# Pinning VectorE operations, five buffers for q, and other queues for some transfers in a four-layer convolution network

## The chip, the cores and the metric

The program runs on one core of one Trainium2 chip. The metric is device time in microseconds from start to end of the program, the median over several executions. Lower is better. All data are float32 except where a table says bf16.

## The reference

Input x is (4, 256, 64, 64). Four layers follow each other, each of the form x + layer(groupnorm(x)); only the first and the preparation of weights for the others concern the change.

```python
# layer 0: axial attention over rows, N = B*H rows, 16 groups, 16 channels each
qkv = einsum('nci,oc->noi', xp, w_qkv)
qkv = bn(qkv)                       # statistics over all rows and positions
qe  = einsum('ngci,cij->ngij', q, q_emb)
ke  = einsum('ngci,cij->ngij', k, k_emb)
qk  = einsum('ngki,ngkj->ngij', qe, ke)
sim = bn(concat([qk, qe, ke]))      # again statistics over everything
sim = softmax(sim summed over its three parts)
attn   = einsum('ngij,ngcj->ngci', sim, v)
attn_e = einsum('ngij,cij->ngci', sim, v_emb)
out = bn(concat([attn, attn_e])) summed in pairs
# layer 1: 3x3 convolution, weights made ternary with a threshold
delta = 0.7 * mean(abs(w));  w_t = where(w > delta, 1, where(w < -delta, -1, 0)) * alpha
# layer 2: two grouped 3x3 convolutions of sign(x), batch norms, residuals
# layer 3: 3x3 convolution whose weights are w * a / (1 + exp(w * b)) for 16 pairs (a, b)
```

## The kernel before

The kernel is written in a tile language. The author writes operations for an engine (VectorE, ScalarE, TensorE, GpSimd, and the queues that issue transfers: SyncE, ScalarE, GpSimd). A scheduler then decides the order of each engine's instructions from estimated durations, mostly the earliest written among those that it holds to be ready, and adds the waits on semaphores. On the chip every engine runs its list in order. A pool hands out tiles; tiles of one tag share so many buffers, and a new tile waits until the last reader of its buffer is done.

The span has three stages ahead of the convolutions.

**Stage A** (the first `with` block, lines 160 to 340) goes over four images b and eight chunks k of 512 positions. `normalised(b)` loads an image in four pieces (SyncE), takes its statistics (L192, VectorE) and yields mean and scale; it is written at chunk 4 of the image before. For each chunk VectorE writes the normalised columns `xg` (L259), TensorE makes q and k rows (`po`, L267) and v columns (`pv`, L282), ScalarE copies them out, VectorE takes statistics of `po` (L274). q and k go to DRAM as `q_d` (L308, SyncE, 16 stores after each image), v as `vt_d` (ScalarE). Beside this the weights of layer 1 are made: `threshold` sums the absolute weights over six pieces (L229), written for b = 0, k = 6; `ternary(i)` (L240 to L250) loads a piece again, compares it (L245, L246), and `kernel_rows` makes six combinations that are stored as `u1_d`, two pieces for each of the images 1 to 3. Both loads and the store are issued by GpSimd, from one buffer.

**Stage B** (lines 365 to 629) goes over 16 tiles j of q and k (4 images, 4 sets of groups). `projections(j)` loads a tile `qb` of 1 MB from `q_d` in two transfers on SyncE (L405) and scales it with four VectorE instructions (L411). There are three buffers; the tile for j + 2 is asked for when tile j begins. A tile takes two group pairs gp, each with four steps: 64 small matmuls `pd` (L446), two VectorE transposes of them into `t` (L453), and, for the step before, 64 small matmuls `pq` (L465) in `product`, copied and squared by ScalarE (L469, L474). After each gp, `term_sums` reduces the tile (L421 to L423), makes a matrix product `ptq` (L426) and multiplies it with the tile (L431), all for batch-norm sums. Between the tiles ten jobs make the weights of layers 3 and 2: `weights_3` (six: exponentials on ScalarE, L488 to L490 and `kernel_rows` on VectorE, a store L496) and `weights_2` (four: loads L502 or L506, sums and splitting into bf16 parts L513 to L522, a store L523). They are written one after each tile from tile 0 on; their transfers are SyncE's.

**Stage C** (lines 633 to 905) goes over eight units. `scores` loads `qc` (L693) and `si` (L711) on SyncE, ScalarE scales qc (L699), TensorE makes `e` (L723), VectorE adds `si` (L735), ScalarE takes exponentials (L765), TensorE sums them (L776) and then makes the values `pa` (L808) and `pe` (L832). `load_values` (L679) fetches the v tiles `vb`, 16 transfers a unit in four parts, each written after the two value products that read the old content; ScalarE issues them.

Of the kernel before, what the change touches and what calls it, by code (L numbers as in the profile page):

```python
# [17 lines left out]
P = 128  # L18
B = 4
# [19 lines left out]
def network(ctx: ExitStack, tc, x, wqkv, relm, relt, relw, relv, counts, masks, vecs, rowv, ab, w1, l2w1, l2w2, l3w, mats, out):  # L39
# [116 lines left out]


    bqh = ctx.enter_context(ExitStack())
    bqp = pool(bqh, "b_q", 3, side="right")
    with ExitStack() as ph:  # L160
        wp = pool(ph, "a_w")
        xp_ = pool(ph, "a_x", 6)
# [57 lines left out]
        delta = sp.tile([P, 2], F32, name="delta")  # L220

        def weights_1(i, name):
            w = kp.tile([P, 3, C], F32, name=f"{name}_{i}", tag="w")
            nc.gpsimd.dma_start(out=w, in_=w1[i])
            return w

        def threshold():
            for i in range(len(pieces)):
                nc.vector.tensor_reduce(  # L229
                    sizes[:, i : i + 1], weights_1(i, "wa").rearrange("p a o -> p (a o)"), AX.X, ALU.add,  # L230
                    apply_absolute_value=True,
                )
            s = small(sp, [P, 1])
            nc.vector.tensor_reduce(s, sizes, AX.X, ALU.add)
            ps = pst.tile([P, 1], F32, name="pdelta", tag="pst")
            nc.tensor.matmul(ps, lhsT=mt[:, M_ALL, :], rhs=s, start=True, stop=True)
            nc.vector.tensor_scalar(delta[:, 0:1], ps, 1.0 / (2 * 9 * C), 0.7, ALU.mult, ALU.mult)
            nc.vector.tensor_scalar(delta[:, 1:2], delta[:, 0:1], -1.0, None, ALU.mult)

        def ternary(i):  # L240
            t, dx = pieces[i]
            w = weights_1(i, "wb")
            alpha = row[:, 96:97]
            up = kp.tile([P, 3, C], F32, name=f"up_{i}", tag="up")
            nc.vector.tensor_scalar(up, w, delta[:, 0:1], alpha, ALU.is_gt, ALU.mult)  # L245
            nc.vector.tensor_scalar(w, w, delta[:, 1:2], alpha, ALU.is_lt, ALU.mult)  # L246
            nc.vector.tensor_tensor(w, up, w, ALU.subtract)
            u = kp.tile([P, 6, C], F32, name=f"u1_{i}", tag="u")
            kernel_rows(u, w, up[:, 0], up[:, 1])
            nc.gpsimd.dma_start(out=u1_d[:, t, dx], in_=u)  # L250

        ready = normalised(0)
        for b in range(B):
            xs, gm, rs = ready
            qs = [qp.tile([P, 8, 8, 64], F32, name=f"qs{t}_{b}", tag="qs") for t in range(2)]
            for k in range(NB):
                xg = gp_.tile([P, 2, 512], F32, name=f"xg_{b}_{k}", tag="xg")
                for t in range(2):
                    nc.vector.tensor_scalar(  # L259
                        xg[:, t, :], xs[t][k // 4][:, bass.ts(k % 4, 512)], gm[:, t : t + 1], rs[:, t : t + 1],  # L260
                        ALU.subtract, ALU.mult,
                    )
                for o in range(2):
                    ps = psp.tile([P, 8, 64], F32, name=f"po_{b}_{k}_{o}", tag="po", bufs=3)
                    psf = ps.rearrange("p h w -> p (h w)")
                    for t in range(2):
                        nc.tensor.matmul(  # L267
                            psf, lhsT=wt[:, t, bass.ts(o, P)], rhs=xg[:, t, :], start=(t == 0), stop=(t == 1)
                        )
                    nc.scalar.copy(  # L270
                        qs[o][:, :, :, bass.ts(k, 8)].rearrange("p l a h -> p h a l"),
                        ps.rearrange("p h (a l) -> p h a l", l=8),
                    )
                    nc.vector.bn_stats(st1[:, o, b * NB + k, :], psf)  # L274
                if k % 2 == 0:
                    vs = vp.tile([P, C, 8], F32, name=f"vs_{b}_{k}", tag="vs")
                for half in range(2):
                    pv = psp.tile([P, 2, C], F32, name=f"pv_{b}_{k}_{half}", tag="pv")
                    for j in range(2):
                        pix = bass.ts(2 * half + j, P)  # L280
                        for t in range(2):
                            nc.tensor.matmul(  # L282
                                pv[:, j, :], lhsT=xg[:, t, pix], rhs=wt[:, t, C : 2 * C],
                                start=(t == 0), stop=(t == 1),
                            )
                    c = 4 * (k % 2) + 2 * half
                    nc.scalar.copy(vs[:, :, c : c + 2], pv.rearrange("p j c -> p c j"))
                    sq = jp.tile([P, 2, C], F32, name=f"vq_{b}_{k}_{half}", tag="vq")
                    nc.scalar.activation(sq, pv, AF.Square)
                    squares.append((b, 2 * k + half, sq))  # L290
                    if len(squares) > 4:
                        for _ in range(4):
                            add_squares()
                if k % 2 == 1:
                    for r in range(2):
                        nc.scalar.dma_start(
                            out=vt_d[b][k // 2, r].rearrange("p a c m -> p a (c m)"),
                            in_=vs.rearrange("p (a r c) m -> p r a (c m)", r=2, c=16)[:, r],
                        )
                if k == 4 and b + 1 < B:  # L300
                    ready = normalised(b + 1)
                if b == 0 and k == 6:
                    threshold()
                if b > 0 and k in (1, 5):
                    ternary(2 * (b - 1) + k // 4)
            for t in range(2):
                for l in range(8):
                    nc.sync.dma_start(  # L308
                        out=q_d[b][l, t].rearrange("c g f -> g c f"), in_=qs[t][:, l].rearrange("p a h -> p (a h)")
                    )  # L310
# [53 lines left out]
    cqp = pool(cih, "c_q", 3)  # L364
    with ExitStack() as ph:
        rp = pool(ph, "b_r")
        tp_ = pool(ph, "b_t", 2)
        op = pool(ph, "b_o", 2)
        jp = pool(ph, "b_j", 2)
# [30 lines left out]
        def projections(j):  # L400

            b, s = divmod(j, 4)
            q = bqp.tile([P, 4, 8, 64], F32, name=f"qb_{j}", tag="qb")
            for t in range(2):
                nc.sync.dma_start(  # L405
                    out=q[64 * t : 64 * t + 64].rearrange("p g a n -> p (g a n)"),
                    in_=q_d[b][:, t, :, 4 * s : 4 * s + 4].rearrange("l c g f -> l c (g f)"),
                )
            for g in range(4):
                c = 4 * s + g  # L410
                nc.vector.tensor_scalar(  # L411
                    q[:, g], q[:, g], sq[:, 0, c : c + 1], sq[:, 1, c : c + 1], ALU.mult, ALU.add
                )
            return q

        def term_sums(j, q, half):

# [63 lines left out]
        def weights_3(t, dx):  # L481
# [11 lines left out]
            u = kp.tile([P, 6, C], F32, name=f"u3_{t}_{dx}", tag="u3")  # L493
            ef = e.rearrange("p r a o -> p (r a o)")
            kernel_rows(u, w, ef[:, 0:C], ef[:, C : 2 * C])
            nc.sync.dma_start(out=u3_d[:, t, dx], in_=u)  # L496

        def weights_2(i, g):

            w = kp.tile([P, 9, 64], F32, name=f"w2_{i}_{g}", tag="w2")  # L500
            if i == 0:
                nc.sync.dma_start(out=w, in_=l2w1[:, g])  # L502
            else:

                for two in range(2):
                    nc.sync.dma_start(out=w[64 * two : 64 * two + 64], in_=l2w2[g][:, two])  # L506
            w3 = w.rearrange("p k o -> p (k o)").rearrange("p (a n) -> p a n", a=3)
            u = kp.tile([P, 4, 3 * 64], F32, name=f"u2_{i}_{g}", tag="u2")
            t = kp.tile([P, 3 * 64], F32, name=f"t2_{i}_{g}", tag="t2")
# [9 lines left out]
            for j in range(3):  # L519
                v.tensor_copy(parts[:, j], uf)  # L520
                if j < 2:
                    v.tensor_tensor(uf, uf, parts[:, j], ALU.subtract)  # L522
            nc.sync.dma_start(out=bk_d[i][:, g], in_=parts)  # L523

        jobs = [(weights_3, (t, dx)) for t in range(2) for dx in range(3)]
        jobs += [(weights_2, (i, g)) for i in range(2) for g in range(2)]
# [17 lines left out]
                whole.append((b, gp, o, 0))  # L544

        last = None
        qs = [projections(0), projections(1)]
        for b in range(B):
            for gp in range(GP):
                j = 4 * b + gp // 2  # L550
                if gp % 2 == 0 and j + 2 < 4 * B:
                    qs.append(projections(j + 2))
                q = qs[0]
                o = op.tile([P, 32, 64, 2], F32, name=f"o_{b}_{gp}", tag="o")
                for nb in range(2):
                    ts = [tp_.tile([P, 16, 64, 2], F32, name=f"t{t}_{b}_{gp}_{nb}", tag=f"t{t}") for t in range(2)]
# [4 lines left out]
                            finish(last, 2 * jh + 1)  # L561
                    last = (ts, o, b, gp, nb)
                term_sums(j, q, gp % 2)
                if gp % 2 == 1:
                    qs.pop(0)
                    if jobs:
                        job, args = jobs.pop(0)
                        job(*args)
        for k in range(4):
# [99 lines left out]
    def attention(general, good):  # L669
# [5 lines left out]
        def load_values(u, m):  # L675
            b, th = units[u]
            for r in range(2):
                for h in range(2):
                    nc.scalar.dma_start(  # L679
                        out=vb[m][64 * r : 64 * r + 64, h, :, 16 * r : 16 * r + 16, :]  # L680
                        .rearrange("p a c m -> p a (c m)"),
                        in_=vt_d[b][m, r, 64 * h : 64 * h + 64, 4 * th : 4 * th + 4]
                        .rearrange("p a c m -> p a (c m)"),
                    )
# [895 lines left out]
```

## Time and profile before

| | |
|---|---|
| time, median of 3 runs | 3115.93 us (3112.61 to 3126.57) |
| span of the profiled execution | 3128.6 us |
| TensorE matmul busy | 2623.8 us (84%) |
| VectorE busy | 2063.7 us (66%) |
| ScalarE busy | 1120.8 us (36%) |
| GpSimd busy | 55.4 us (2%) |
| moved by DMA | 484.05 MB, mean 155 GB/s |

In the profile PE is TensorE's matmul, PEld its weight load, DVE VectorE, ACT ScalarE, POOL GpSimd, SP SyncE; a q behind a name (SPq, ACTq) is the engine's queue of instructions that issue transfers. L411 is line 411 of the kernel. A row of a timeline gives the start and the duration in us, engine, line, operation, output <- input, the number of merged instructions, and in brackets the idle time of the engine before it with what ended it. A row of waits names the waiting engine and line, who released it, the total in us, how often, and the longest.

### The profile page before, as it was taken

Reading aid. Unit: us, or ns where it says so; the run is one execution under the profiler, and the core shown is the slowest. Engines: PE = TensorE matmul, PEld = TensorE weight load, DVE = VectorE, ACT = ScalarE, POOL = GpSimd, SP = SyncE. Lnnn points to the kernel's source line nnn. Section 1 sums busy time; section 2 is a strip of 40 time slices with the busy share of each in tenths; the row PEclk is TensorE's granted clock in tenths of the full one; section 3 lists DMA queues with packets and bytes.
Section 4 is the critical chain, followed back from the end, with each engine's and each line's share of the span. In section 5 each row is a group of like instructions: output and inputs, shape, how many; then the busy total and the mean of one; then the engine's idle time right before and its main releaser. Section 6 shows DMA issues by size and latency. Waiting matters only on the chain. (4 is left out here: it accounts for less than half of the span.)

```text
span 3128.6 us, 82568 instructions
## 1 busy us (share of the span) xinstructions
PE 2623.8 (84%) x36800; PEld 1593.2 (51%) x36800; DVE 2063.7 (66%) x3554; ACT 1120.8 (36%) x2201; POOL 55.4 (2%) x119
## 2 busy tenths in 40 slices
PE   5789778878888777777773699999996885999998
PEld 3456556656666656655663344444453452444443
DVE  5653897655655545555566888877597768778653
ACT  2445344444445465555541010101267931101010
POOL 0000000000000000000000000000000000000000
PEclk9989889889889988999997899999998997999999
DMA  5765354333233567776766444340434644443200
GB/s 187 246 202 158 120 193 154 116 110 128 107 110 124 145 198 236 249 246 227 243 206 225 127 155 151 102 151 28 158 121 166 233 165 151 134 133 116 88 40 41
DMA packets 246522, 484.05 MB, mean 155 GB/s; under 512 B 27344, under 2 KB 127056, under 8 KB 226320
## 3 DMA queue, kind: packets, MB, share of 16 engines
q1 hardware_dynamic: 147872, 335.02, 32.5%
q10 hardware_dynamic: 96464, 134.24, 12.3%
q0 software_dynamic: 1824, 9.44, 0.9%
q8 instruction: 291, 4.77, 0.6%
q14 instruction: 71, 0.58, 0.1%
HBM read 282.28 MB, written 196.35 MB: 153 GB/s over the span
## 5 line engine op out<-in xcount | busy, mean ns | idle before, releaser
L971 PE MATMUL gc<-gtr,g_u 128*128 128x512 f32 x1152 | 500.2, 596 | 21.2 <-issue 13.0
L971 PE MATMUL dc<-dtr,d_u 128*128 128x512 f32 x1152 | 502.7, 597 | 17.6 <-DVE dtr L957 12.0
L446 PE MATMUL pd<-rm,qb 64*32 64x256 f32 x8192 | 296.8, 408 | 92.5 <-DVE t L453 87.7
L453 DVE STREAM_TRANSPOSE t<-pd 128x1024 f32<-128x1024 f32 x256 | 304.4, 1226 | 102.0 <-PE pd L446 101.1
L971 PEld LDWEIGHTS gc<-gtr,g_u 128*128 128x128 f32 x1152 | 218.1, 190 | 295.4 <-issue 281.7
L971 PEld LDWEIGHTS dc<-dtr,d_u 128*128 128x128 f32 x1152 | 217.4, 190 | 288.8 <-issue 264.5
L465 PEld LDWEIGHTS pq<-t,t 64*64 64x64 f32 x8192 | 266.0, 139 | 81.9 <-issue 52.4
L465 PE MATMUL pq<-t,t 64*64 64x64 f32 x8192 | 285.3, 223 | 24.5 <-issue 17.3
L1203 PE MATMUL pc<-e_tr,e_k 128*64 128x512 bf16 x2304 | 266.0, 392 | 38.6 <-ACT pc_o L1211 19.9
L469 ACT ACTIVATE o<-pq 128x512 f32<-128x512 f32 x256 | 152.2, 595 | 390.2 <-PE pq L465 389.9
L446 PEld LDWEIGHTS pd<-rm,qb 64*32 64x32 f32 x8192 | 161.9, 113 | 180.5 <-DVE t L453 102.5
L765 ACT ACTIVATE pt<-pt,sm 128x512 f32<-128x512 f32 x256 | 162.5, 708 | 188.8 <-DVE pt L735 111.4
L1203 PEld LDWEIGHTS <-e_k 128*64 128x64 bf16 x2304 | 152.2, 112 | 151.2 <-issue 49.6
L735 DVE TENSOR_TENSOR pt<-e_False,si_False 128x1024 f32<-128x1024 f32 x128 | 150.5, 1217 | 60.7 <-PE e_False L723 60.6
L776 PE MATMUL den_False<-pt,cnt 128*32 128x128 f32 x2048 | 118.3, 302 | 55.9 <-ACT pt L765 32.4
L474 ACT ACTIVATE pq<-pq 128x512 f32<-128x512 f32 x256 | 149.5, 584 | 5.9
L267 PE MATMUL po<-xg,wt 128*128 128x512 f32 x256 | 126.3, 633 | 23.4 <-DVE st L274 20.3
L989 ACT COPY gc_c<-gc 128x512 f32<-128x512 f32 x32 | 18.6, 581 | 343.8 <-PE gc L971 343.8
L989 ACT COPY dc_c<-dc 128x512 f32<-128x512 f32 x32 | 18.7, 584 | 329.2 <-PE dc L971 329.2
L723 PE MATMUL e_False<-qc_False,rw 32*64 32x256 f32 x2048 | 111.5, 422 | 21.9 <-ACT qc_False L699 11.9
L808 PE MATMUL pa_False<-pt,vb 128*32 128x64 f32 x4096 | 103.0, 240 | 27.5 <-issue 23.0
L832 PE MATMUL pe_False<-pt,ve 128*32 128x64 f32 x4096 | 91.3, 233 | 39.6 <-issue 33.0
(379 smaller groups left out, 3437.5 us busy)
## 6 DMA issues: line engine op xcount, KB each, us to landing
si_False<-qk_d SPq DMA_DIRECT2D x64, 1024.0 KB
qk_d<-o ACTq DMA_DIRECT2D x124, 512.0 KB
x<-x_d SPq DMA_DIRECT2D x32, 1056.0 KB
a<-at_d SPq DMA_DIRECT2D x256, 128.0 KB
xa<-in_x SPq DMA_DIRECT2D x16, 1024.0 KB
vt_d<-vs ACTq DMA_DIRECT2D x32, 512.0 KB
q_d<-qs SPq DMA_DIRECT2D x64, 256.0 KB
qb<-q_d SPq DMA_DIRECT2D x32, 512.0 KB
```

The costliest lines, as they stand in the source:

```text
L267: nc.tensor.matmul(psf, lhsT=wt[:, t, bass.ts(o, P)], rhs=xg[:, t, :], start=(t == 0), stop=(t == 1))
L446: nc.tensor.matmul(pds[t][32 * c : 32 * c + 32, m].rearrange("p j k -> p (j k)"), lhsT=q[rows, 2 * (gp % 2) + g, a, 32 * nb : 32 * nb + 32 ...
L453: nc.vector.transpose(ts[t][:, :, 32 * jh : 32 * jh + 32].rearrange("p a j b -> p j a b"), pds[t].rearrange("p m j k -> p j m k"),)
L465: nc.tensor.matmul(ps[rows, m, :], lhsT=ts[1][rows, n // 2, :, n % 2], rhs=ts[0][rows, n // 2, :, n % 2], start=True, stop=True, tile_posi ...
L469: nc.scalar.activation(o[:, :, 8 * k : 8 * k + 8, :], ps.rearrange("p n (a b) -> p a n b", b=2), AF.Copy, accum_out=acc[:, 0, gp, col : co ...
L474: nc.scalar.activation(psf, psf, AF.Square, accum_out=acc[:, 1, gp, col : col + 1])
L723: nc.tensor.matmul(es[x_ // 2][64 * r : 64 * r + 64, x_ % 2, :, :, par], lhsT=rw[rows, par, 63 - i : 127 - i], rhs=q[rows, :, k % 2, :].re ...
L735: nc.vector.tensor_tensor(dst, e, src, ALU.add)
L765: nc.scalar.activation(s, s, AF.Exp, scale=s2q[:, gp : gp + 1])
L776: nc.tensor.matmul(dens[u, h][32 * a : 32 * a + 32], lhsT=ones[:, i, :], rhs=pt[:, 16 * h + i, a].rearrange("p n b -> p (n b)"), start=(i ...
L971: nc.tensor.matmul(ms[k], lhsT=u[:, t, dx, k, bass.ts(co, P)], rhs=vs[t][:, k, :, dx : dx + 64], start=(first and dx == 0), stop=(last and ...
L1203: nc.tensor.matmul(m[64 * g : 64 * g + 64], lhsT=parts[:, g, i, k, dx, :], rhs=vs[g][:, k, 8 * (q % 2) : 8 * (q % 2) + 8, dx : dx + 64], s ...
```

## The change

The change touches stages A, B and C; what is computed stays.

- **Pins.** `tc.keep_in_program_order` holds a VectorE instruction at its written place in the engine's order. It is put around the four scalings of a q tile, the six reductions for the threshold, and the first comparison of each ternary piece.
- **q tiles.** Five pools of one buffer each, used by turns, in place of one pool of three; two of the five lie in stage B's own memory. Loads are asked for three tiles ahead, and the scaling of tile j + 1 is written in the middle of tile j, after `term_sums` of its first half.
- **Layer 1's weights.** Each reduction is written for its own chunk (k = 2 to 7 of image 0), the pieces have two buffers and are loaded by SyncE; those for `ternary` are loaded two chunks ahead of their use.
- **Weights of layers 2 and 3.** Their jobs begin after tile 3 rather than tile 0, and their loads and stores in the loop are issued by GpSimd.
- **Value loads** of stage C are issued by SyncE.

It is meant to keep VectorE from standing in front of a load, and the queues of SyncE and ScalarE from standing in front of transfers that wait.

```diff
-    bqp = pool(bqh, "b_q", 3, side="right")
+    bqps = [pool(bqh, f"b_q{i}", side="right") for i in range(3)]
...
         def weights_1(i, name):
-            w = kp.tile([P, 3, C], F32, name=f"{name}_{i}", tag="w")
-            nc.gpsimd.dma_start(out=w, in_=w1[i])
+            w = kp.tile([P, 3, C], F32, name=f"{name}_{i}", tag="w", bufs=2)
+            nc.sync.dma_start(out=w, in_=w1[i])
             return w
-        def threshold():
-            for i in range(len(pieces)):
+        def threshold(i):
+            w = weights_1(i, "wa")
+            tc.keep_in_program_order(
                 nc.vector.tensor_reduce(
-                    sizes[:, i : i + 1], weights_1(i, "wa").rearrange("p a o -> p (a o)"), AX.X, ALU.add,
+                    sizes[:, i : i + 1], w.rearrange("p a o -> p (a o)"), AX.X, ALU.add,
                     apply_absolute_value=True,
                 )
+            )
+            if i + 1 < len(pieces):
+                return
...
+        pieces_1 = {}
         def ternary(i):
-            w = weights_1(i, "wb")
+            w = pieces_1[i]
...
-            nc.vector.tensor_scalar(up, w, delta[:, 0:1], alpha, ALU.is_gt, ALU.mult)
+            tc.keep_in_program_order(
+                nc.vector.tensor_scalar(up, w, delta[:, 0:1], alpha, ALU.is_gt, ALU.mult)
+            )
...
-                if b == 0 and k == 6:
-                    threshold()
+                if b == 0 and 1 < k:
+                    threshold(k - 2)
                 if b > 0 and k in (1, 5):
                     ternary(2 * (b - 1) + k // 4)
+                if k in (3, 7) and 2 * b + k // 4 - 1 in range(len(pieces)):
+                    i = 2 * b + k // 4 - 1
+                    pieces_1[i] = weights_1(i, "wb")
...
+        bqps += [pool(ph, f"b_q{i}") for i in range(3, 5)]
...
-            q = bqp.tile([P, 4, 8, 64], F32, name=f"qb_{j}", tag="qb")
+            q = bqps[j % 5].tile([P, 4, 8, 64], F32, name=f"qb_{j}", tag="qb")
...
+            return q
+        def scaled(j, q):
             for g in range(4):
-                c = 4 * s + g
-                nc.vector.tensor_scalar(
-                    q[:, g], q[:, g], sq[:, 0, c : c + 1], sq[:, 1, c : c + 1], ALU.mult, ALU.add
+                c = 4 * (j % 4) + g
+                tc.keep_in_program_order(
+                    nc.vector.tensor_scalar(
+                        q[:, g], q[:, g], sq[:, 0, c : c + 1], sq[:, 1, c : c + 1], ALU.mult, ALU.add
+                    )
                 )
-            return q
...
-            nc.sync.dma_start(out=u3_d[:, t, dx], in_=u)
+            nc.gpsimd.dma_start(out=u3_d[:, t, dx], in_=u)
...
-                nc.sync.dma_start(out=w, in_=l2w1[:, g])
+                nc.gpsimd.dma_start(out=w, in_=l2w1[:, g])
...
-                    nc.sync.dma_start(out=w[64 * two : 64 * two + 64], in_=l2w2[g][:, two])
+                    nc.gpsimd.dma_start(out=w[64 * two : 64 * two + 64], in_=l2w2[g][:, two])
...
-            nc.sync.dma_start(out=bk_d[i][:, g], in_=parts)
+            nc.gpsimd.dma_start(out=bk_d[i][:, g], in_=parts)
...
-        qs = [projections(0), projections(1)]
+        qs = [projections(j) for j in range(3)]
+        scaled(0, qs[0])
         for b in range(B):
             for gp in range(GP):
                 j = 4 * b + gp // 2
-                if gp % 2 == 0 and j + 2 < 4 * B:
-                    qs.append(projections(j + 2))
-                q = qs[0]
+                if gp % 2 == 0 and j + 3 < 4 * B:
+                    qs.append(projections(j + 3))
+                q = qs[j]
...
                 term_sums(j, q, gp % 2)
+                if gp % 2 == 0 and j + 1 < 4 * B:
+                    scaled(j + 1, qs[j + 1])
                 if gp % 2 == 1:
-                    qs.pop(0)
-                    if jobs:
+                    if j > 2 and jobs:
                         job, args = jobs.pop(0)
                         job(*args)
...
-                    nc.scalar.dma_start(
+                    nc.sync.dma_start(
                         out=vb[m][64 * r : 64 * r + 64, h, :, 16 * r : 16 * r + 16, :]
```

## The prediction

> **What bounds the kernel now.** I read the page first (PE 84% busy, DVE 66%: neither is full), then cut the span by the first and last start of each line's instructions: stage A (projections of x) 0 to 333.6 us, stage B (position terms, products) 333.6 to 1076.9, stage C (attention) to 1690, then the convolutions, which the change leaves alone. All is decided in A to C, so I asked for the waits and stretches there. First the waits of stage B (waiting engine and line, releaser: us in total, times, longest), then those of SyncE's queue:
>
> ```profile
> PEld pd L446 <- DVE t L453: 102.5, 29, 9.0
> DVE t L453 <- PE pd L446: 101.1, 81, 2.5
> DVE qb L411 <- DMA qb<-q_d: 100.3, 13, 9.6
> PE pd L446 <- DVE t L453: 87.7, 25, 8.5
> ...
> SPq L405 <- DVE pr L431: 352.6, 13, 45.4
> SPq L496 <- DVE u L153: 66.1, 4, 24.7
> ```
>
> TensorE waits for transposes (L453), VectorE for the load of q (L411), and the load for a free buffer, which the last `pr` of tile j-1 gives back. VectorE is in order, so transposes queue behind the waiting scaling. The timeline shows one such round:
>
> ```profile
> 629.74 2.38 DVE L453 STREAM_TRANSPOSE t<-pd 128x1024 f32<-128x1024 f32 x2 [0.48 <-PE pd L446]
> 641.72 1.91 DVE L411 TENSOR_SCALAR qb<-qb,sm 128x512 f32<-128x512 f32 x4 [9.60 <-DMA qb<-q_d]
> ...
> 638.50 1.17 PE L465 MATMUL pq<-t,t 64*64 64x64 f32 x31 [3.74 <-issue]
> 644.85 3.65 PE L446 MATMUL pd<-rm,qb 64*32 64x256 f32 x60 [4.37 <-DVE t L453]
> ```
>
> The load is issued at 629.34 and lands 12 us later; after the gap 60 matmuls take 3.65 us, elsewhere 64 take 1.96. What a round costs is seen in the stretches: a tile with a load, and one of the last three, whose scaling is done:
>
> ```profile
> 688.60:735.20 46.60, 37.46 (x1040) 28.78 (x1040) 26.28 (x42) 20.91 (x64) 0.00 (x0) 0.90 0.33 115
> 1001.60:1037.00 35.40, 35.40 (x1044) 27.96 (x1041) 21.91 (x33) 20.91 (x64) 0.00 (x0) 1.00 0.32 122
> ```
>
> (us, then busy PE, PEld, DVE, ACT, POOL, granted clock.) Without the wait PE is full. In stage A, VectorE waits for weight pieces, and at 209 for x, and PE with it:
>
> ```profile
> 30.18 0.95 DVE L229 TENSOR_REDUCE sizes<-wa 128x1 f32<-128x768 f32 x1 [4.00 <-DMA wa<-in_w]
> ...
> 126.05 0.68 DVE L245 TENSOR_SCALAR up<-wb,delta,row 128x768 f32<-128x768 f32 x1 [9.64 <-DMA wb<-in_w]
> 149.81 0.68 DVE L245 TENSOR_SCALAR up<-wb,delta,row 128x768 f32<-128x768 f32 x1 [6.63 <-DMA wb<-in_w]
> 209.34 1.88 DVE L192 BATCH_NORM_STATS2 sm<-xa 128x6 f32<-128x512 f32 x3 [14.68 <-DMA xa<-in_x]
> ...
> 134.51 3.75 PE L267 MATMUL po<-xg,wt 128*128 128x512 f32 x4 [9.59 <-DVE st L274]
> 157.34 0.59 PE L118 MATMUL pst<-sm,mt 128*128 128x2 f32 x2 [6.46 <-DVE sm L110]
> 216.20 3.78 PE L267 MATMUL po<-xg,wt 128*128 128x512 f32 x4 [10.10 <-DVE st L274]
> ```
>
> L229 is written for the seventh chunk of image 0 and ran at 9 to 40 us: the scheduler moves ready-looking work ahead. In stage C ScalarE issues the value loads:
>
> ```profile
> 1081.34 15.06 ACTq L679 DMA_DIRECT2D vb<-vt_d  x15
> 1096.45 9.34 ACT L699 ACTIVATE qc_False<-qc_False,sm 128x128 f32<-128x128 f32 x24 [14.87 <-DMA vb<-vt_d]
> ...
> 1245.57 2.56 ACT L765 ACTIVATE pt<-pt,sm 128x512 f32<-128x512 f32 x4 [19.07 <-DMA vb<-vt_d]
> ...
> 1243.20 2.34 DVE L735 TENSOR_TENSOR pt<-e_False,si_False 128x1024 f32<-128x1024 f32 x2
> ```
>
> The first pays 15 us. The second looks like 19, but the sum it needs (L735) ended at 1245.54: there the load issue costs nothing.
>
> **What the Trainium skill says.** "TensorE: Matmul & The Clock Gate", Part 1, has the array fall to half clock after an idle window of about 3.4 us; the 3.65 us above agree. "DMA: Bandwidth & Descriptors", Issuing engines are not separate DMA queues: a transfer does not get faster on another queue, only the issuer's time is saved. So the moved stores and loads count here only by who stands behind them in a queue. "Runtime: NRT & Kernel Launch", Instruction fetch mechanics: each sequencer fetches its instructions by DMA in blocks, mostly hidden. Here less so: five of the 13 q loads have an "issue" gap of PE beside them, of 2.2 to 4.5 us.
>
> **Stage B, part by part.** Five buffers and loads three tiles ahead: tile j+1's load is now issued at about the start of j-2 and needed in mid j, 50 us or more for a 12 us transfer; weight stores no longer stand before it on SyncE. The scaling, pinned behind `term_sums` of the tile before, should find its data. Floor: from ptq to ptq at full clock the trace has 997.24 - 979.50 = 17.74 us for half a tile, x32 = 568, plus 4 for entry and tail: 572. It takes 743 now, so 171 us lie above the floor. What comes back:
> - Weight work. It runs at 346 to 480 us now, with VectorE full. Its rows in stage B sum to about 89 us: six weights_3 of some 11.5 us (four reciprocals at 1.34, four L488 and L490 at 0.2 and 0.4, then kernel_rows 3.9), four weights_2 of 5. It now goes to tiles 3 to 12. A tile needs 26.3 us of VectorE (stretch above); with weights_3 37.8, over the 35.5 PE needs. VectorE in its full stretch (350 to 400 us) was busy 47.6 of 50, so 37.8 / 0.95 = 39.8: 4.3 x 6 = 26, and 1 each for weights_2: 30. Bounds 14 (perfect packing, 2.3 x 6) and 50 (8 x 6 and 2).
> - Instruction fetch. PE was active for some 7 of each load's 12 us, and met a gap of about 3.7 in 5 of 13; over all 12 us that is 0.65 x 3.7 x 13 = 31. In tiles where VectorE is the limit a part is hidden: 25. Bounds 5 and 45.
> - The 1.9 us scaling now sits just before a pair of transposes. These have 1.57 us of slack a step: 0.5 a tile, 7. Bounds 0 and 20.
> Sum 62, so stage B takes 634: 109 us saved, between 56 and 152.
>
> **Stage A.** Gains: 5 at the start (statistics ended at 26.2, L195 ran at 31.05 behind the reduction), 6.5 for the gap at 157, and 3 of the 9.6 at 134, since x landed only at 133 and takes over as the releaser. The gap at 216 is for x, stays. Costs: weight pieces now stand on SyncE between x loads and q_d stores (these were issued over 22 us at 177 to 200), and a pinned instruction that waits holds xg and all statistics behind it, for which PE waits. Two buffers and loads two chunks (14 us) ahead hide most of it; no row shows the new wait, so I take 6, between 0 and 25. Net 8, between -10 and 20.
>
> **Stage C.** The 15 issues leave ScalarE; PE's wait there was 11.9 us: 12 saved, between 8 and 15. In later units the value loads go out on SyncE between its si loads (1214.7 and 1245.9), in an empty stretch: nothing either way. Weight stores and loads on GpSimd (55 us busy in all) cost nothing: it has no other work in stage B.
>
> Sum: 109 + 8 + 12 = 129; 3116 - 129 = 2987.
>
> **Rivals.**
> 1. VectorE becomes the bound of stage B: the weight operations bunch in front of transposes and PE also meets every fetch gap. The 101 us in which VectorE waits for PE speak against it, the full stretch at 350 to 480 for it. Saving 56 + 0 + 10: 3050.
> 2. Weight work and fetch fit the slack (after all VectorE needs 510 us of 572): 152 + 15 + 14 saved, 2935.
> 3. Slower: a pin holds VectorE for loads that come late on SyncE. Twelve pinned weight operations at the 6 us of now's wait are 72 us of stage A, and if the scalings still wait nothing is gained in B: 3116 + 72 - 12 = 3176. Against it: the load's lead of 50 us in B, 14 in A.
> 4. The gain of B is given back in A and C: about 3116. Nothing in the profile speaks for it.
>
> **Numbers.** Forecast 0.58, rival 1 0.17, rival 2 0.15, rival 3 0.07, rival 4 0.03. The predicted time is 2987. Low end: 152 + 20 + 15 saved, 2929, taken as 2925; high end: 56 - 10 + 8 = 54 saved, 3062, taken as 3065; about 1 in 10 lies outside on the slow side and less below. Faster 0.90, same 0.03, slower 0.07.
>
> **What would show it.** Right: no wait of L411 for its load, tiles of 35 to 37 us without weight work and about 40 with, L453 no longer the first releaser of L446 in tiles without it, ScalarE's first L699 near 1082 less the shift. Wrong: L411 waiting for qb or TensorE for L453 in every tile, or waits of L229 or L245 above 5 us in stage A. If the marked instructions turn out to be fences for all others, statistics of the next image wait for x in front of a pin, and stage A grows.

## The result and the profile after

| | before | after |
|---|---|---|
| time, median of 4 | 3114.27 us (3107.18 to 3126.57) | 3030.6 us (3000.26 to 3045.38) |
| ratio, 95% interval | | 0.9695 (0.9603 to 0.9786) |
| span of the profiled execution | 3128.6 | 3043.6 |

By the medians the kernel is about 84 us faster. The ratio, here and in the tables below, leaves out executions more than 1.5% above the fastest of their kernel, which medians, ranges and the stage times of `after` (its profiled execution, at 3045.38 us, was the longest of the four) keep. Where the time came from is read by cutting both spans at the same events: stage A to the first `pd`, stage B to the last `pq`, stage C to the last `pa`. Stretches of the kernel before (us, then busy PE, PEld, DVE, ACT, POOL, granted clock, DMA share, GB/s):

```profile
0.00:333.60 333.60, 264.32 (x1098) 167.78 (x1098) 164.08 (x365) 138.00 (x198) 13.14 (x23) 0.94 0.64 201
333.60:1077.00 743.40, 627.08 (x16644) 474.46 (x16644) 495.83 (x844) 346.27 (x1054) 3.79 (x4) 0.91 0.36 125
1077.00:1690.00 613.00, 452.64 (x14354) 347.80 (x14354) 338.71 (x459) 297.97 (x554) 35.58 (x68) 0.91 0.70 224
1690.00:3128.60 1438.60, 1279.81 (x4704) 603.13 (x4704) 1065.03 (x1889) 338.51 (x396) 2.85 (x24) 0.95 0.38 130
```

The same of the kernel after:

```profile
0.00:298.90 298.90, 263.11 (x1098) 167.53 (x1098) 163.83 (x365) 139.32 (x200) 4.20 (x11) 0.96 0.72 225
298.90:1011.00 712.10, 622.72 (x16644) 470.10 (x16644) 497.06 (x845) 347.84 (x1056) 16.78 (x23) 0.95 0.38 132
1011.00:1608.00 597.00, 450.27 (x14333) 349.34 (x14336) 339.12 (x459) 296.28 (x550) 32.59 (x66) 0.90 0.70 228
1608.00:3043.60 1435.60, 1279.06 (x4740) 603.18 (x4731) 1065.79 (x1889) 338.42 (x396) 2.85 (x24) 0.95 0.38 130
```

Stage A gave 35 us where 8 were forecast, stage B 31 where 109 were (33 by the exact cut used in the tables below, with stage C at 14), stage C 16 where 12 were. The total is 85 of the forecast 129. So one stage was read far too low and one far too high.

**Stage B after.** Its waits (waiting engine and line, releaser: us in total, times, longest):

```profile
DVE t L469 <- PE pd L462: 153.7, 78, 8.3
PEld pd L462 <- DVE t L469: 68.5, 37, 10.0
...
PEld pq L481 <- issue: 59.1, 94, 4.7
...
PE pd L462 <- DVE t L469: 51.1, 35, 9.6
...
PEld pd L462 <- issue: 37.7, 86, 4.6
```

The wait of the scaling for its load (100.3 us before, L427 now) is in no row: it is gone. VectorE now waits for TensorE (101.1 before, 153.7 after), so VectorE is no longer what holds TensorE up in most tiles: of the 51.1 us that TensorE's matmuls still wait for transposes, 36.8 lie in the first four tiles, before 500.6, and then it is one wait of 1.3 us a tile. Yet TensorE is not full. What has grown is "issue", time in which it waited for nothing that the profile shows (52.4 and 32.3 before). One tile in the timeline:

```profile
698.97 1.91 DVE L427 TENSOR_SCALAR qb<-qb,sm 128x512 f32<-128x512 f32 x4
...
702.06 2.37 DVE L469 STREAM_TRANSPOSE t<-pd 128x1024 f32<-128x1024 f32 x2
703.36 1.96 PE L462 MATMUL pd<-rm,qb 64*32 64x256 f32 x62 [1.30 <-DVE t L469]
...
718.78 1.20 SPq L417 DMA_DIRECT2D qb<-q_d  x2
...
730.00 2.80 PE L462 MATMUL pd<-rm,qb 64*32 64x256 f32 x45 [3.91 <-issue]
```

Two things cost time here. The four scalings (1.91 us) stand before a pair of transposes, and TensorE waits 1.30 us. And 7 us after the load for a later tile was issued at 718.78, TensorE stands for 3.91 us, and 45 matmuls then take 2.80 us where 64 take 1.96. Such a gap of over 2 us comes nine times in stage B of after, five times before. Eight of the nine end 8 to 12 us after the issue of a load of q; the ninth, at 902.28, has none beside it. Three tiles as stretches, with weight work, with a load, without either:

```profile
375.90:427.70 51.80, 41.35 (x1040) 29.42 (x1038) 51.64 (x100) 24.06 (x74) 4.02 (x7) 0.97 0.54 183
...
699.00:743.40 44.40, 39.20 (x1050) 29.75 (x1040) 26.40 (x45) 20.93 (x64) 0.00 (x0) 0.92 0.35 121
...
830.00:867.40 37.40, 36.10 (x1048) 28.19 (x1040) 26.42 (x45) 21.00 (x64) 0.00 (x0) 1.00 0.31 120
```

The first has VectorE busy for 51.64 of 51.80 us. The jobs for the weights are written after tiles 3 to 12, and the scheduler ran all of them between 300 and 469 us, most of them in tiles 1 to 3: the pins hold the marked instructions in place, not the unmarked ones around them. The second has VectorE at 26.40 of 44.40 us, so it isn't the bound; the clock is 0.92.

**Stage A after.** The timeline:

```profile
5.83 7.51 DVE L192 BATCH_NORM_STATS2 sm<-xa 128x6 f32<-128x512 f32 x12 [5.83 <-DMA xa<-in_x]
...
16.27 0.37 DVE L195 BATCH_NORM_AGGREGATE sm<-sm 128x2 f32<-128x48 f32 x1
...
110.35 3.25 PE L275 MATMUL po<-xg,wt 128*128 128x512 f32 x4 [2.89 <-DVE st L282]
133.77 0.58 PE L118 MATMUL pst<-sm,mt 128*128 128x2 f32 x2 [7.12 <-DVE sm L110]
```

and of before, rows from the same beginning:

```profile
9.13 0.95 DVE L229 TENSOR_REDUCE sizes<-wa 128x1 f32<-128x768 f32 x1 [9.13 <-DMA wa<-in_w]
10.00 2.46 DVE L192 BATCH_NORM_STATS2 sm<-xa 128x6 f32<-128x512 f32 x4
17.02 0.95 DVE L229 TENSOR_REDUCE sizes<-wa 128x1 f32<-128x768 f32 x1 [4.55 <-DMA wa<-in_w]
...
31.05 0.36 DVE L195 BATCH_NORM_AGGREGATE sm<-sm 128x2 f32<-128x48 f32 x1
```

The first statistics start at 5.83 instead of 10.00, and the mean is there at 16.27 instead of 31.05. In before VectorE stood three times at a reduction whose weight piece had not landed, with the statistics behind it in its order: 9.13, 4.55 and the 4.00 us that the prediction shows, 17.7 in all. Now it waits once, 5.83 us, and for x. The first product `po` moves from 36.3 to 20.2 us. That is 16 of the 35 us; TensorE's gap of 9.59 is now 2.89, that of 6.46 is 7.12, and that of 10.10 is 2.9. The pinned comparisons (L252) and reductions (L230, now at 43 to 81 us) never waited.

**Stage C after.** Timeline:

```profile
1004.07 17.63 SPq L697 DMA_DIRECT2D vb<-vt_d  x16
...
1020.30 9.34 ACT L717 ACTIVATE qc_False<-qc_False,sm 128x128 f32<-128x128 f32 x24 [6.12 <-DVE sm L366]
...
1027.94 0.39 SPq L729 DMA_DIRECT2D si_False<-qk_d  x1
```

ScalarE is free of the issues. Its first scaling comes 9.3 us after the stage's start instead of 19.5; but now SyncE stands 17.63 us in the issues, and the first further load of `si` leaves only at 1027.94.

### The profile page after: what moved, and what is told of

Same layout as the page of the kernel before. It is cut to its first block, busy times and chain, and to the rows that moved or that the text cites. A ratio compares the mean times of both kernels' runs of the same rounds, so it can differ in the third digit from the quotient of the medians.

```text
span 3043.6 us, 82578 instructions
## 1 busy us (share of the span) xinstructions
PE 2615.2 (86%) x36800; PEld 1590.2 (52%) x36800; DVE 2065.8 (68%) x3554; ACT 1121.8 (37%) x2201; POOL 56.4 (2%) x123
## 5 line engine op out<-in xcount | busy, mean ns | idle before, releaser
L469 DVE STREAM_TRANSPOSE t<-pd 128x1024 f32<-128x1024 f32 x256 | 304.2, 1227 | 153.7 <-PE pd L462 153.7
L462 PE MATMUL pd<-rm,qb 64*32 64x256 f32 x8192 | 291.5, 396 | 67.2 <-DVE t L469 51.1
L741 PE MATMUL e_False<-qc_False,rw 32*64 32x256 f32 x2048 | 122.8, 427 | 26.1 <-DVE pt L753 15.9
L794 PE MATMUL den_False<-pt,cnt 128*32 128x128 f32 x2048 | 100.5, 299 | 50.4 <-issue 25.3
L290 PE MATMUL pv<-wt,xg 128*128 128x256 f32 x512 | 120.8, 384 | 0.0
```

What stands on the lines that cost most here:

```text
L290: nc.tensor.matmul(pv[:, j, :], lhsT=xg[:, t, pix], rhs=wt[:, t, C : 2 * C], start=(t == 0), stop=(t == 1),)
L462: nc.tensor.matmul(pds[t][32 * c : 32 * c + 32, m].rearrange("p j k -> p (j k)"), lhsT=q[rows, 2 * (gp % 2) + g, a, 32 * nb : 32 * nb + 32 ...
L469: nc.vector.transpose(ts[t][:, :, 32 * jh : 32 * jh + 32].rearrange("p a j b -> p j a b"), pds[t].rearrange("p m j k -> p j m k"),)
L741: nc.tensor.matmul(es[x_ // 2][64 * r : 64 * r + 64, x_ % 2, :, :, par], lhsT=rw[rows, par, 63 - i : 127 - i], rhs=q[rows, :, k % 2, :].re ...
```

## The experiments

In the tables stage times are cut as above, and "gaps" counts TensorE's issue gaps of over 2 us in stage B. Times are medians, with the ratio to the kernel before on the same chip. Three chips were used, one for each group; the kernel after differed by chip, 0.9792 on the first and 0.9693 on the third, so ratios are compared within a group.

### Each stage's part of the change alone

`a_only` is the kernel before with the hunks of stage A, `c_only` with those of stage C, and `b_only` is the kernel after with both undone:

```diff
 # a_only: before, and
+                if b == 0 and 1 < k:
+                    threshold(k - 2)
...
+                    pieces_1[i] = weights_1(i, "wb")
 # c_only: before, and
-                    nc.scalar.dma_start(
+                    nc.sync.dma_start(
                         out=vb[m][64 * r : 64 * r + 64, h, :, 16 * r : 16 * r + 16, :]
```

> The kernel before with stage A's part alone: pinned reductions and comparisons, weight pieces loaded by SyncE into two buffers. Theory (the parts add up, each in its stage): stage A ends near 299 us rather than 333.6, the first chunk's matmul starts near 20 us rather than 36, stages B and C keep their 743 and 613 us; about 35 us below the kernel before. Rival (the early start only shifts waits of stage B, or stage A's gain comes from the five q buffers and the other memory layout): less than 15 us below.

> The kernel before with stage B's part alone: pinned scalings one tile ahead, five buffers, weight jobs from tile 3, weight transfers by GpSimd. Theory (the parts add up): stage B near 712 us rather than 743, no wait of the scaling for its load, but tiles with a load at 42 to 45 us and the first three at 52; about 31 us below the kernel before. Rival (stage B was held back by the changes in stage A): stage B at 640 or less, 100 us below.

> The kernel before with the value loads issued by SyncE, nothing else. Theory: ScalarE scales qc some 9 to 12 us sooner at the start of stage C and the later units keep their times; 10 to 16 us below the kernel before, stage C near 597 us. Rival (ScalarE's issuing cost something in each of the eight units): 25 us or more. Second rival (SyncE's loads of si stand behind the value loads): no gain.

> The changed kernel itself, for the same chip as the three parts. Theory (the parts add up): the sum of the three gains, 80 to 90 us below the kernel before. Rival (they share a gain): the sum of the three single gains is over 110 us.

| | A | B | C | gaps | time | ratio (95%) |
|---|---|---|---|---|---|---|
| before (profile above) | 333.7 | 744.4 | 612.9 | 5 | 3131.77 | |
| a_only | 298.9 | 747.9 | 609.2 | 6 | 3099.01 | 0.9906 (0.9875 to 0.9937) |
| b_only | 332.7 | 721.2 | 612.9 | 9 | 3089.61 | 0.9872 (0.9837 to 0.9908) |
| c_only | 336.7 | 744.3 | 613.7 | 6 | 3134.31 | 1.0018 (0.9975 to 1.0061) |
| after_again | 298.5 | 716.0 | 620.0 | 8 | 3065.57 | 0.9792 (0.9759 to 0.9825) |

The parts add up within the noise: 33 + 42 - 3 = 72 us by the medians of the three against 66 of the whole, for which 80 to 90 had been expected. Stage A's 35 us are its own. Stage B's part brings 23 us of stage B in its profile, whose execution, at 3103.5 us, was the longest of the four. For stage C's part no gain is seen: the low end of its interval is 0.9975, 8 us, and 12 had been forecast. In its profile ScalarE does come earlier:

```profile
1081.96 16.37 SPq L679 DMA_DIRECT2D vb<-vt_d  x16
...
1091.00 9.34 ACT L699 ACTIVATE qc_False<-qc_False,sm 128x128 f32<-128x128 f32 x24 [6.11 <-DVE sm L355]
...
1093.85 2.37 PE L723 MATMUL e_False<-qc_False,rw 32*64 32x256 f32 x32 [3.11 <-ACT qc_False L699]
```

TensorE's wait for that scaling fell from 11.9 us to 3.11, but the stage took 613.7 against 612.9. The lead was not lost where SyncE stands in the issues: the first `pa` comes 56.1 us after the stage's start against 64.8, and five sixths through the 4096 `pa` the lead is still 6 us (504 against 510). It goes in the last sixth. TensorE's issue gaps within the stage summed to 95.4 us against 87.1. Stage C of the kernel after alone came out at 599, 620 and 606 in three profiles, so why those 9 us went is not settled by one profile, nor is the 14 to 16 us that the first profile of after shows in stage C a gain.

### Which loss holds stage B: the loads, the place of the scalings, the weight jobs

Four kernels, each the kernel after with one edit. `no_loads` leaves out the loads of tiles 5 to 15 of q and uses the tiles already loaded, so most of stage B works on other numbers. `pieces` loads the same bytes in eight transfers with rows of 2 KB, in place of two with rows of 8 KB. `spread_scales` puts one scaling after each of the four steps of a half tile. `parts` cuts the weight jobs into small pieces, pins the first instruction of each, and writes one after every second step.

```diff
 # no_loads
-                    qs.append(projections(j + 3))
+                    qs.append(projections(j + 3) if j < 2 else qs[j - 2])
 # pieces
-                nc.sync.dma_start(
-                    out=q[64 * t : 64 * t + 64].rearrange("p g a n -> p (g a n)"),
-                    in_=q_d[b][:, t, :, 4 * s : 4 * s + 4].rearrange("l c g f -> l c (g f)"),
-                )
+                for g in range(4):
+                    nc.sync.dma_start(
+                        out=q[64 * t : 64 * t + 64, g].rearrange("p a n -> p (a n)"),
+                        in_=q_d[b][:, t, :, 4 * s + g],
+                    )
 # spread_scales
-                if gp % 2 == 0 and j + 1 < 4 * B:
-                    scaled(j + 1, qs[j + 1])
...
                         position_terms(q, ts, gp, nb, jh, f"{b}_{gp}_{nb}")
+                        if gp % 2 == 1 and j + 1 < 4 * B:
+                            g = 2 * nb + jh
+                            scaled(j + 1, qs[j + 1], range(g, g + 1))
 # parts
-                    if j > 2 and jobs:
-                        job, args = jobs.pop(0)
-                        job(*args)
...
                         position_terms(q, ts, gp, nb, jh, f"{b}_{gp}_{nb}")
+                        next_part()
```

> The changed kernel, with tiles 5 to 15 of q not loaded: they take the tiles of five before (the transfers are left out and the values differ; every instruction of the engines stays). Theory (fetch: while a q load is under way TensorE's instructions come late, 4 us and a stretch at half clock each time): the gaps of TensorE marked issue of over 2 us in stage B go from eleven to at most three, the tiles after the weight work go from 42 to 45 us to about 37.4, stage B falls by 50 to 60 us. Rival (the gaps are due to the stores of qk_d or to TensorE's own fetch rate): gaps and tile times stay, under 10 us gained.

> The changed kernel with each q tile loaded in eight transfers of one group each, rows of 2 KB, rather than two of 8 KB rows; same bytes. Theory (a fetch stands behind the long rows queued on its DMA engine): gaps get shorter, 1 to 2 us rather than 3.5 to 4.6, and stage B falls by 20 to 45 us. Rival (it is the amount of bytes, or any traffic at all): gaps as before, under 10 us either way.

> The changed kernel with the four scalings of the next tile pinned one after each of the four steps of the tile's second half, rather than all four before the first of them. Theory (1.9 us of scalings in front of a transpose pair exceed the slack of a step, one of 0.5 us does not): the 1.3 us wait of TensorE for the transpose after each scaling goes, a tile without load goes from 37.4 to 35.5 us, 20 to 28 us gained over 15 tiles. Rival (the lost time moves to the next step): under 8 us.

> The changed kernel with the weight jobs of layers 2 and 3 cut in some 50 parts of about 2 us of VectorE each, their first instruction pinned, one part after every second step of tiles 1 to 14. Theory (the scheduler still moved the jobs to the first three tiles, where VectorE is full; spread, they fit its idle time): the first three tiles go from 52 to under 45 us and the others grow by at most 2, stage B falls by 25 to 45 us. Rival (VectorE's work for them delays transposes wherever it stands): under 10 us.

| | B | gaps | time (range) | ratio (95%) |
|---|---|---|---|---|
| after (first profile) | 711.5 | 9 | | |
| no_loads | 666.2 | 2 | 3003.88 (2997.39 to 3016.24) | 0.9616 (0.9584 to 0.9648) |
| pieces | 666.8 | 0 | 3000.34 (2995.06 to 3006.84) | 0.9593 (0.9573 to 0.9612) |
| spread_scales | | 8 | 2994.72 (2985.97 to 3032.35) | 0.9571 (0.9541 to 0.9601) |
| parts | | 14 | 3022.3 (2976.7 to 3042.17) | 0.9592 (0.9509 to 0.9674) |

The profiled executions of `spread_scales` and `parts` were the longest of theirs by 30 and 17 us (3032.35 and 3042.17), so no stage time is taken from them. The kernel after was not run on the chip of this group; its row is from the first profile. Stage B as a stretch of `no_loads`:

```profile
296.20:962.40 666.20, 605.91 (x16644) 462.08 (x16644) 496.84 (x843) 347.17 (x1054) 16.27 (x23) 0.98 0.34 124
```

and of `pieces`:

```profile
290.50:957.30 666.80, 607.02 (x16644) 462.31 (x16644) 496.61 (x843) 347.29 (x1054) 16.29 (x23) 0.99 0.39 142
```

Both end 45 us below after (50 to 60 had been expected of `no_loads`, 20 to 45 of `pieces`), with the clock up from 0.95 to 0.98 and 0.99. No loads and loads in short rows are worth the same, so it is not the bytes that cost: it is the form of the transfer. Length of rows and number of transfers were changed together, so which of the two counts is not shown. The queue of these transfers in the page of after (queue, packets, MB, share of 16 engines):

```profile
q1 hardware_dynamic: 182368, 348.27, 35.2%
```

and of `pieces`:

```profile
q1 hardware_dynamic: 189280, 348.27, 35.2%
```

Same bytes and same share of the engines, in 6912 more packets. What TensorE stands for in the gaps can be read from another queue of the page of after:

```profile
q8 instruction: 291, 4.77, 0.6%
```

Its packets are 16 KB each, and 131 of the 291 start in stage B, one for every 254 of the 33288 instructions that TensorE has there (16644 matmuls and as many weight loads, in the stretch above), so they bring TensorE's. Their times in the trace show the fetch. From 500 us on they start 5.0 us apart in the median, and nine times over 7 us apart, each time in front of one of the nine gaps. So it is beside the load issued at 718.78: the 8 KB packets of this load run from 720.14 to 729.98, and no instruction packet starts between 717.28 and 727.31. That one lands at 728.51, and TensorE goes on at 730.00. All eleven issue gaps of over 1 us in stage B of after end 1.4 to 1.6 us after such a packet has landed, those of the other runs 1.2 to 1.8; of all matmuls in stage B of after only 8% start 1.3 to 1.7 us after one. In `pieces`, over the same stretch, no two of these packets start more than 6.8 us apart. So TensorE stood for instructions that came late, and they came late because their packet started late. In front of the ninth gap it is not long rows that are under way, but 8192 packets of 64 bytes, for a table of stage C, from 890.42 to 898.47; the instruction packet starts at 899.72.

That the instruction packet stands behind the load's packets on its DMA engine is argued. "DMA: Bandwidth & Descriptors", section Queues, rings and completion order, in the Trainium skill has each DMA engine change between its rings only after a whole packet, which fits. The trace doesn't say which engine a packet took, so no run here shows the standing itself.

`spread_scales` took away the waits behind the scalings, as in this half tile, where the step after a scaling has no idle time:

```profile
699.34 0.50 DVE L427 TENSOR_SCALAR qb<-qb,sm 128x512 f32<-128x512 f32 x1
700.99 2.38 DVE L469 STREAM_TRANSPOSE t<-pd 128x1024 f32<-128x1024 f32 x2 [1.15 <-PE pd L462]
```

VectorE waits 1.15 us for TensorE there, and not the other way round. `parts` missed its forecast of under 45 us for the first tiles: tiles 1 to 3 take 42 to 47 us, with gaps beside them. What this edit and `parts` are worth is measured better in the next group.

### All three, and the load's form in the kernel before

`all3` joins `pieces`, `spread_scales` and `parts`; `pieces_spread` leaves out `parts`; `before_pieces` is the kernel before with the diff of `pieces` alone; `after_third` is the kernel after again.

> The kernel after, with all three repairs at once: the q load in eight transfers with 2 KB rows, one scaling after each of four steps, and the weight jobs in small parts between the steps. If the three losses of stage B are separate (issue gaps about 46 us, scalings in front of a transpose pair about 25, bunched weight jobs about 14), they add up: stage B from 711 to about 625, no issue gap of PE over 2 us in it, the first tiles near 42 us and the late ones near 36, time about 2945 to 2965, ratio to the kernel before 0.94 to 0.95. Rival: they hide one another (a tile is bound either by VectorE or by the gap), so that together they bring little more than the best of them: stage B 650 to 665, ratio about 0.955.

> As all3, without the weight jobs in parts. If the losses are separate: stage B about 640, the first tiles with a weight job still near 50 us, the others near 36, ratio 0.945 to 0.95; the difference to all3 is what bunching of the weight jobs costs once the rest is gone, 10 to 20 us. If bunching is hidden by then, it equals all3.

> The kernel before with nothing changed but the q load in eight transfers with 2 KB rows. Theory: the wait of the scaling (L411) comes from the buffer that is given back late, and stays; only the issue gaps of PE beside the loads go, some 20 to 45 us of stage B (744 to about 700 to 725), and the wait of L411 for qb stays above 60 us in sum. Rival: the slow transfer with long rows is the cause of the wait too; then L411's wait falls below 40 us, stage B goes to 650 to 670, and the buffers and pins were not needed for it.

> The kernel after, unchanged, on the chip of the other three, as the measure for them: ratio to the kernel before 0.965 to 0.98, stage A near 298, stage B 710 to 716, stage C between 599 and 620.

| | A | B | C | gaps | time | ratio (95%) |
|---|---|---|---|---|---|---|
| before | | | | | 3122.37 | |
| before_pieces | 331.3 | 711.6 | 603.7 | 0 | 3081.34 | 0.9870 (0.9842 to 0.9898) |
| after_third | 296.2 | 713.1 | 605.9 | 9 | 3028.11 | 0.9693 (0.9667 to 0.9719) |
| pieces_spread | 291.4 | 649.2 | 607.1 | 0 | 2979.52 | 0.9540 (0.9513 to 0.9567) |
| all3 | 292.5 | 640.2 | 602.4 | 6 | 2970.83 | 0.9508 (0.9483 to 0.9533) |

`all3` beats both kernels: 57 us under after, 152 under before. It missed its own forecast of 625 in stage B by 15 (`pieces_spread` its 640 by 9), and six issue gaps of 2.2 to 2.9 us were back. They point to the same cause. Two of them in its timeline:

```profile
515.96 0.53 POOL L533 DMA_DIRECT2D u_d<-u  x1 [57.64 <-DVE u L168]
524.11 1.05 PE L498 MATMUL pq<-t,t 64*64 64x64 f32 x27 [2.50 <-issue]
...
857.84 0.54 POOL L562 DMA_DIRECT2D bk_d<-k  x1 [39.46 <-DVE k L559]
866.77 0.21 PE L498 MATMUL pq<-t,t 64*64 64x64 f32 x1 [2.16 <-issue]
```

Each of the six ends 6.5 to 9.6 us after the issue of a store of made weights, which has rows of 6 KB (768 KB from 128 partitions) or 4.5 KB (576 KB); four of the ten stores have no gap over 2 us. That these rows make the gaps was not tried by cutting them. One after the other, the repairs bring 45 us of stage B for the form of the load (711.5 to 666.8), 18 for the scalings (to 649.2) and 9 for the weight jobs in pieces (to 640.2). Such a chain gives the whole (73 us from `after_third` to `all3`) in any case, so it doesn't show that the losses are separate; the three edits alone came out alike (0.9593, 0.9571, 0.9592), on a chip on which after was not run. By medians the gain is smaller, 49 us for `pieces_spread` and 57 for `all3`: the profiled execution of `after_third`, at 3051.55 us, is the longest of its six.

Tiles of `pieces_spread` with weight work, and two after it:

```profile
371.80:424.00 52.20, 40.95 (x1040) 30.18 (x1032) 50.94 (x101) 24.08 (x74) 3.77 (x7) 0.96 0.62 215
...
467.40:503.40 36.00, 36.00 (x1055) 28.21 (x1040) 26.34 (x44) 20.82 (x66) 0.00 (x0) 1.00 0.41 150
503.40:541.80 38.40, 36.22 (x1052) 28.29 (x1040) 26.35 (x43) 21.07 (x65) 0.00 (x0) 1.00 0.38 141
```

A tile with VectorE full is still 52.2 us; the others are between 35.9 and 39.1. In `all3` a tile with much VectorE work and its neighbour read:

```profile
353.70:393.00 39.30, 37.18 (x1055) 28.41 (x1040) 34.37 (x61) 22.39 (x69) 0.00 (x0) 1.00 0.60 214
393.00:432.50 39.50, 37.85 (x1056) 28.49 (x1048) 31.85 (x53) 20.95 (x66) 0.53 (x1) 1.00 0.42 159
```

Here VectorE has 31.9 to 34.4 us of work in tiles of some 39 us, and no tile has it full.

`before_pieces` is the surprise: an edit of five lines gives stage B what the buffers, pins and queues of the change gave it (711.6 against 711.5). The round that the prediction showed of before looks like this:

```profile
625.95 0.55 DVE L412 TENSOR_SCALAR qb<-qb,sm 128x512 f32<-128x512 f32 x1 [4.40 <-DMA qb<-q_d]
...
631.18 3.66 PE L447 MATMUL pd<-rm,qb 64*32 64x256 f32 x62 [5.53 <-DVE t L454]
```

and in its waits

```profile
DVE qb L412 <- DMA qb<-q_d: 58.1, 27, 5.6
```

The wait for the load fell from 100.3 to 58.1 us: neither above 60 (the late buffer alone) nor below 40 (the slow transfer alone). The first scaling starts 7.2 us after the first issue of the load, at 618.76, instead of 12, and after a wait of 5.53 us the next 62 matmuls still take 3.66 us. So both reasons share the wait. Stage B in the four combinations: long rows 744.4 before and 711.5 after, short rows 711.6 and 666.8. The change is worth 33 us of stage B with long rows and 45 with short ones.

## Why the prediction was right in time and wrong in its parts

**The wait for the load** went as forecast: no row of L427 for its DMA, load far ahead, no new wait on a pin. The first reason of the forecast holds, and rival 3, the pin that waits, is refuted.

**Stage B: 109 forecast, between 56 and 152; 33 by the cut, below the range.** Three terms of its sum failed; one held, in sum.
- Weight work, forecast 30: in `pieces_spread` three tiles of 51.5, 52.2 and 43.4 us stand against 37.7, the mean of the others: 13.8 + 14.5 + 5.7 = 34. That the sum held is luck in part: the jobs ran in the first four tiles, with VectorE full in two of them, not at some 40 us a tile in tiles 3 to 12, and 9 us come back by spreading. The trace of before had the sign: jobs written after tiles 0 to 9 had all run by 519 us, in the first four tiles.
- "Instruction fetch", 25: the right mechanism, mis-sized; the form of the load costs 45, the upper bound named. The step had some eight or nine gaps at 3.7 us, and nine were met, 30 us in sum; the three loads in the bunched tiles met none, as it had it. But the half clock after a gap was not in the sum: TensorE is busy 622.72 us in stage B of after and 607.02 in that of `pieces`.
- The scaling before a pair of transposes, 7: it cost 18. The step charged half a microsecond a tile, for 1.91 us of scaling against 1.57 us of slack; the row shows TensorE waiting 1.30 us, in 15 tiles.
- The floor of 572 came from one half tile near the end of stage B, which has no load beside it. With the form of the load and the scalings repaired, the eleven tiles of `pieces_spread` without weight work take 36 to 39 us, 37.7 on the mean, against 35.4: 2.3 x 16 = 37 us over the floor. That term was missing. It isn't the load: the last three of the eleven, after the last load of q, take 36.1, 39.1 and 36.9. In these tiles TensorE is busy for 36 to 37 us. A part of the rest is issue gaps of under 1.3 us, 13.6 us over stage B; the other part stays open.

Sum: 572 + 34 + 45 + 18 = 669, and 43 more for the missing term and what remains: the 712 measured.

**Stage A: 8 forecast, between -10 and 20; 35 measured, above the range, and `a_only` shows it is its own.** The step "5 at the start" was mis-sized: 16. It read only the last of the three waits in front of the mean (26.2 to 31.05), not those of 9.13 and 4.55 us before it, which the rows above show. This is read from the two traces; the reductions and their loads were not tried apart. The gap at 216 "stays" was wrong too (10.10 to 2.9; the wait of VectorE for x before it went from 14.68 to 6.22 us, why is open). The gap of 9.59 gave 6.7 where 3 was taken, that of 6.46, which was to go, stayed at 7.12, and the 6 charged for pinned waits was 0.

**Stage C: 12 forecast, not shown.** TensorE's wait shrank by 8.8 us as the step said, but `c_only` is equal to before within its interval. The step took it that a lead at the start of the stage is kept to its end; in `c_only` it was lost in the last sixth of the value products, and not where SyncE issues 16 loads in 16 us ahead of `si`. Why stays open.

So the time lay in the range by luck: stage A gave 27 us more than forecast while stage B fell 76 short, both outside the bounds set for them. The 3030.6 measured is 44 us from the forecast and 19 from rival 1 (3050), which had VectorE full and every gap met: true of two tiles, and of the gaps, but VectorE waits for TensorE in the rest.

## What to carry to other kernels

Before giving a load more buffers and an earlier issue, look at what stands beside it: here the form of the transfer (two with 8 KB rows, or eight with 2 KB rows) cost as much of stage B as all that the buffers, pins and queues repaired there, 33 us each in the kernel before, and the two repairs add. If TensorE stands and waits for nothing that the profile names, look when its instruction packets started and landed. A pin on an instruction holds that instruction; work that is written for later and isn't pinned may still be moved into the stretch that was to be kept free. Take a floor from the mean of several tiles rather than from one good half tile, and check for each stage apart whether the forecast held, since a total can be right by two errors.

## What the hardware showed unexpectedly

- A 1 MB load as two transfers with 8 KB rows left TensorE without instructions for 2.4 to 4.6 us, beside eight of the eleven loads that are issued within stage B of after; as eight with 2 KB rows, the same bytes and DMA share, for at most 1.8 us (`pieces`, `pieces_spread`, `before_pieces`). "Runtime: NRT & Kernel Launch" in the Trainium skill, Instruction fetch mechanics, calls this fetch "mostly hidden"; here it left 30 us of gaps of over 2 us in stage B of after.
- A gap of 3.91 us cost the next 45 matmuls double the time (2.80 us, at the full rate 1.38); one of 1.30 us cost the next 62 nothing (1.96). One of 2.79 us, shorter than the 3.4 us of the prediction, cost the next 58 some 1.4 us, since 64 of them take 2.14 elsewhere:

```profile
643.41 3.36 PE L481 MATMUL pq<-t,t 64*64 64x64 f32 x58 [2.79 <-issue]
```
